# A decoder layer on one core: its first block done by batch entry, its first latents without transfers

## The chip, the cores and the metric

The kernel runs on one NeuronCore of a Trainium2 chip. The metric is device time in microseconds of one execution; lower is better. The engines are TensorE (PE: matmuls; its weight loads are shown as PEld), VectorE (DVE), ScalarE (ACT) and GpSimd (POOL). Each takes its instructions strictly in the order in which they were issued, and they meet through semaphores. Most DMA transfers are issued by SyncE (SP), also in order; a few are issued by ScalarE.

## The reference

One decoder layer over x of 32 batch entries, 256 tokens, 256 features, all float32. In short:

```python
x = x + attn(layernorm(x))               # causal self attention
x = x + xattn(layernorm(x), ctx, mask)   # cross attention
x = x + ffn(layernorm(x))                # relu, fp8-quantised hidden values
```

Self attention goes through latents: `q = (x @ Wqa @ Wqb)` with 64 latents, `kv = (x @ Wkva @ Wkvb)` with 32, 16 query heads of 16 features, 4 key and value heads, rotary positions on q and k, a causal softmax, then `@ Wout + bout`. Cross attention takes keys and values from `ctx`, 16 heads of 16 features, and a mask of 256 x 256. Scores are held to float32 accuracy: operands are split into a rounded high half and a low remainder ("halves"), each multiplied for itself.

## The kernel before

The 32 batch entries are worked on two at a time: 16 blocks (i = 0 to 15) of 512 tokens. Each block has a self attention (a0, a1, ...), a cross attention (x0, x1, ...) and a feed-forward part. An attention is a job of 8 units; a unit is one batch entry b and one group g of four heads. The jobs run one behind the other: a0, a1, x0, a2, x1, a3, ... , a15, x14, x15. So between a0 and x0 there is only a1 to cover a0's output projection, norm, transposes and x0's queries.

The order of instructions is written out by hand. Time is counted in steps, one unit to a step: at step s the maxima of unit s are computed (`row_max`: scores by TensorE, masked maximum by VectorE, line 400), two units earlier is weighted (`weigh`: scores again with the maximum subtracted; `exponential` on ScalarE; for self attention GpSimd zeroes the upper triangle), and every second step the values of an earlier pair are summed (`values`, copied to `num`, and spread by `gather`: denominators to `den`, outputs to `oT`). Dense work is hung between them by `at(pos, fn, rank)`, where pos is a step in halves, and rank 1 comes after rank 0. All engines and SP's queue follow this one order.

An attention's units run g outside and b inside, unless the job stands in `APART`; then b is outside, so that the first four units need only batch entry 0. `APART` held a15, x14 and x15. For i = 15 the tail of the self attention is then also done by entry (`divide_entry`, `tr_entry`, `xquery_entry`, `queries_entry`), for the other blocks over both entries at once (`divide`, `tr`, `xquery`, `queries`).

The path in front of the first scores: x of block 0 is loaded; `Norm.moments` (VectorE, then GpSimd), `Norm.scaled` (ScalarE), transposes to `xnT` (`tr`), and `lat`: one product with `wa_sb` gives 96 rows of latents, ScalarE copies them to `rlat` and rounds them, GpSimd makes the low halves, and six SP transfers spread them over 128 partitions as `lk` and `lq` (lines 680 and 684). `rotated` multiplies by the weights with rotary pairs (`rope`: TensorE, VectorE line 349, GpSimd line 350), `split` makes halves again (lines 335 and 336), and `keys` and `queries` spread them by transfers (`spread`, line 294) to the tiles that the units read. For a0 the second of each two groups is issued by ScalarE, the rest by SP. Each of the 512 tokens of the block goes through each of these in one piece.

Tiles come from small rings: `hl` (halves) has three buffers, `r` and `t` two, the PSUM pool of dense work two banks, that of the scores three pairs; `lk`, `lq`, `xn` and `den` have one buffer each.

Positions of block 0: the load at -16, moments -14 and -13.5, norm -13 and -12.5, transposes -12, latents -11, keys -9 and 0.5, queries -8 and 1.5 (each for one half of the features, both entries), values 2.5; reciprocal of the denominators 11.5, divide 12.5, output projection 13 and 13.5, norm 13.5 and 14, transposes 14.5, x0's queries 15 and 15.5, x0 itself from 16.

Of the kernel before, what the change touches and what calls it, by code (L numbers as in the profile page):

```python
# [10 lines left out]
F32 = mybir.dt.float32  # L11
F32R = mybir.dt.float32r
# [5 lines left out]
ALU = mybir.AluOpType  # L18
# [23 lines left out]
def decoder_layer(  # L42
# [3 lines left out]
    w_a, w_q, w_k, w_v, w_out, b_out,  # L46
# [25 lines left out]
    def load(name, src):  # L72
        return fetch(const.tile(list(src.shape), src.dtype, name=name), src)
# [18 lines left out]
    wa_sb = load("wa_sb", w_a)  # L92
    bout_sb = load("bout_sb", b_out)
# [4 lines left out]
    low_sb = load("low_sb", low)  # L98
    ones2_f = fetch(sm.tile([P, 2, P], F32, tag="nmT", name="ones2_f"), ones2)
# [14 lines left out]
    def latent_weights():  # L114

        nc.scalar.copy(wq_s[0], wq_f)
        nc.gpsimd.tensor_tensor(wq_s[1], wq_f, wq_s[0].bitcast(F32), ALU.subtract)
        for w, f in ((wk_s, wk_f), (wv_s, wv_f)):
            hi = sm.tile(list(f.shape), F32R, tag="t", name="hi_w")
            nc.scalar.copy(hi, f)  # L120
            nc.vector.scalar_tensor_tensor(w, hi.bitcast(F32), low_sb, f, ALU.mult, ALU.add)

    def score_constants():


        nc.vector.tensor_copy(ones2_sb, ones2_f)
        nc.gpsimd.tensor_copy(sel_sb, sel_f)

        tri_f = sm.tile([P, S], F32, tag="t", name="tri_f")
        nc.gpsimd.memset(tri_f, 0.0)  # L130
        nc.gpsimd.affine_select(
            out=tri_f, in_=tri_f, compare_op=ALU.is_ge, fill=NEG_CAUSAL,
            base=P, pattern=[[-1, S]], channel_multiplier=1,
        )
        nc.vector.tensor_copy(causal_qk, tri_f)

# [154 lines left out]
    def spread(job, t, part, e):  # L291

        queue = nc.scalar if job.first and e == 1 else nc.sync
        queue.dma_start(out=t, in_=part[e * 64 : (e + 1) * 64])

    def queries(job, c, hl):

        for e in range(2):
            g = 2 * c + e
            t = act.tile([P, TOK], F32R, tag=f"q{g}{job.set}", name=f"q{g}_{job.name}", bufs=1)  # L300
            rows = t.bitcast(F32).rearrange("(r s) t -> s r t", s=2)
            for s in range(2):
                spread(job, rows[s], hl[:, s, :].bitcast(F32), e)
            job.q[g] = t
# [15 lines left out]
    def keys(job, c, hl):  # L320

        for e in range(2):
            g = 2 * c + e
            t = act.tile([P, 2, TOK], F32R, tag=f"k{g}{job.set}", name=f"k{g}_{job.name}", bufs=1)
            rows = t.bitcast(F32).rearrange("(r s) h t -> s r h t", s=2)
            for s in range(2):
                spread(job, rows[s], hl.bitcast(F32), e)
            job.k[g] = [t[:, h, :] for h in range(2)]
# [4 lines left out]
    def split(name, r, n=P):  # L333
        hl = halves(name)
        nc.scalar.copy(hl[:n, 0, :], r[:n])
        nc.gpsimd.tensor_tensor(hl[:n, 1, :], r[:n], hl[:n, 0, :].bitcast(F32), ALU.subtract)  # L336
        return hl
# [25 lines left out]
    class Job:  # L363
        def __init__(self, name, n, causal, apart):
            self.apart = apart
            self.units = [(g, b) for b in range(2) for g in range(G)] if apart else [
                (g, b) for g in range(G) for b in range(2)
            ]
            self.name, self.set, self.causal, self.first = name, n % 2, causal, n == 0
            self.q, self.k = {}, {}  # L370
            self.mx, self.nmT, self.wT = {}, {}, {}
# [176 lines left out]
    APART = {("a", NI - 1), ("x", NI - 2), ("x", NI - 1)}  # L548
# [17 lines left out]
    def entries(i):  # L566
# [28 lines left out]
        def tr(name):  # L595
# [5 lines left out]
            return run  # L601

# [205 lines left out]
        if i == 0:  # L808
            p = dict(load=-16, m=(-14, -13.5), n=(-13, -12.5), tr=-12, lat=-11, k=(-9, 0.5), q=(-8, 1.5), v=2.5)
        elif i == 1:  # L810
# [5 lines left out]
        at(s0 + p["load"], load)  # L816
        for c in range(2):
            ln("a", c, s0 + p["m"][c], s0 + p["n"][c], s0 + p["n"][c])
        at(s0 + p["tr"], tr("a"))
        at(s0 + p["lat"], lat)  # L820
        for c in range(EC):
            for kind in "kq":
                rotated(kind, c, s0 + p[kind][c])
        at(s0 + p["v"], value)

        if i in (0, NI - 1):
            p = dict(inv=11.5, div=(12.5, 12.5), o=(13, 13.5), n=(13.5, 14), tr=14.5, q=(-1, -0.5), k=(-5, -4), ctx=-8, v=(3.5, 4))
            if i == NI - 1:
                p.update(inv=(8, 12), div=(9.5, 13.5), o=(10.5, 14.5), n=(11.5, 15.5), tr=(12, 16), q=(-3, 1), k=(-7, -1))
            if i == 0:  # L830
                p.update(ctx=-13, v=(-2, 0))
# [26 lines left out]
        if jx.apart:  # L858
# [26 lines left out]
    at(-11.5, latent_weights)  # L885
    at(-9.5, score_constants)
# [62 lines left out]
def _constants():  # L949
# [12 lines left out]
    low = np.zeros((P, 1), np.float32)  # L962
    low[2 * KVL :] = -1.0
# [6 lines left out]
def _layout(a):  # L970
# [6 lines left out]
        "w_a": _chunks(np.concatenate([a["L0_attn_Wqa"], a["L0_attn_Wkva"]], axis=1)),  # L977
        "w_q": np.tile(_both(a["L0_attn_Wqb"]), (2, 1, 1)),
# [38 lines left out]
```

## Time and profile before

| | us |
|---|---|
| median of three runs | 1688.2 (1687.71 to 1691.75) |
| the profiled execution | 1687.51 |
| its span, from first to last instruction | 1685.8 |
| first scores on TensorE | 33.36 |
| first masked maximum of a0, a1, x0, a2 | 34.6, 89.9, 164.3, 208.5 |
| the next jobs, each | 46.9 to 48.6 |
| granted TensorE clock, mean | 0.951 |

A page of the profile has busy times of each engine, and forty slices of the span in which a digit is the busy share in tenths; `PEclk` is the clock that TensorE was granted, in tenths of full speed. A line of the timeline has the start, the duration, the engine (`SPq` is SP's queue), the line of the kernel, the operation, the tile written and those read, the shape, how many in a row, and in brackets how long the engine had been idle and what ended that. A line of waits has the engine, the tile and line that waited, what it waited for, the total in us, how often, and the longest. The span is 2.4 us shorter than the median.

### The profile page before, as it was taken

The page shows a single profiled execution, that of the slowest core. Times are in us where ns is not written, and L with a number is a line of the kernel's source. Part 1 is how long each engine was busy: PE and PEld are TensorE (multiplying, and loading weights), DVE is VectorE, ACT ScalarE, POOL GpSimd, SP SyncE. Part 2 cuts the span into 40 slices and gives each one's busy share as a digit, 9 for nine tenths or more (in the row PEclk, how much of TensorE's full clock was granted, in tenths as well). Part 3 has the DMA queues.
Part 4 walks back from the last instruction along what each step waited for, and adds up shares of the span by engine and source line. Part 5 has one row for each costly group of instructions (what it writes and reads, how often), then busy time and mean ns, then how long its engine had stood idle before and what let it go on. Part 6 is the DMA issues. An engine that isn't in the chain of part 4 may idle for free. (4 is left out here: it accounts for less than half of the span.)

```text
span 1685.8 us, 47975 instructions
## 1 busy us (share of the span) xinstructions
PE 1540.7 (91%) x17748; PEld 1002.2 (59%) x17748; DVE 1291.0 (77%) x5083; ACT 964.2 (57%) x1545; POOL 1099.8 (65%) x1862
## 2 busy tenths in 40 slices
PE   3777899999999999999999999999999999989886
PEld 2444566665656566665656566665656566555664
DVE  3554978979797888879787887878787887957861
ACT  2343566666665666666566666656566666545542
POOL 5655576776867677685867677675867677555521
PEclk7687799999999999999999999999999999999898
DMA  4533234252434335242434325243434425131200
GB/s 137 169 97 95 78 84 129 62 136 66 113 92 125 96 77 149 65 125 77 114 86 125 102 68 158 59 110 96 114 90 114 112 63 135 52 89 46 61 18 22
DMA packets 85738, 160.42 MB, mean 95 GB/s; under 512 B 15296, under 2 KB 36160, under 8 KB 85376
## 3 DMA queue, kind: packets, MB, share of 16 engines
q1 hardware_dynamic: 84864, 155.78, 34.6%
q8 instruction: 140, 2.29, 0.6%
q10 hardware_dynamic: 640, 1.57, 0.3%
q14 instruction: 94, 0.77, 0.1%
HBM read 22.03 MB, written 8.39 MB: 18 GB/s over the span
## 5 line engine op out<-in xcount | busy, mean ns | idle before, releaser
L400 DVE CUSTOM_DVE_ANT_0 ms_x<-s_x,mb_qk 128x256 f32<-128x256 f32 x1024 | 362.0, 417 | 64.2 <-POOL hl_q L336 23.9
L400 DVE CUSTOM_DVE_ANT_0 ms_a<-s_a,causal_qk 128x128 f32<-128x128 f32 (+1 forms) x1024 | 294.3, 352 | 61.3 <-PE s_a L389 17.8
L430 DVE TENSOR_TENSOR wT_x<-wT_x,cap_kq 128x1024 f32<-128x1024 f32 x256 | 303.4, 1225 | 0.0
L455 ACT ACTIVATE wT_x<-s_x 128x1024 f32<-128x1024 f32 x256 | 248.3, 1023 | 30.5 <-PE s_x L442 30.2
L405 POOL CAST maxima<-m_x 128x8 fp32r<-128x8 f32 x128 | 115.6, 903 | 214.7 <-DVE m_x L400 113.2
L775 PE MATMUL ps_h<-xnT_f,w_sb 128*128 128x512 f32 x448 | 221.4, 616 | 0.0
L455 ACT ACTIVATE wT_a<-s_a 128x768 f32<-128x768 f32 x256 | 193.3, 807 | 23.5 <-PE s_a L442 19.5
L461 POOL TENSOR_SCALAR_AFFINE_SELECT wT_a<-wT_a 128x256 f32<-128x256 f32 x512 | 191.6, 411 | 21.2 <-ACT wT_a L455 21.1
L389 PE MATMUL s_a<-k_a,q_a 32*128 32x128 f32 (+1 forms) x2048 | 115.8, 314 | 35.1 <-ACT wT_a L455 19.5
L442 PEld LDWEIGHTS s_a<-q_a,k_a 32*128 32x128 f32 x2048 | 86.6, 189 | 80.3 <-issue 66.4
L779 ACT ACTIVATE hq<-ps_h,b_sb 128x512 fp8e4<-128x512 f32 x112 | 77.1, 689 | 91.6 <-PE ps_h L775 91.6
L479 PE MATMUL av_x<-wT_x,v_cross 128*32 128x256 f32 x2048 | 129.2, 393 | 0.0
L389 PE MATMUL s_x<-k_x,q_x 32*128 32x256 f32 x2048 | 111.4, 311 | 17.9 <-ACT wT_x L455 8.8
L442 PEld LDWEIGHTS s_x<-q_x,k_x 32*128 32x128 f32 x2048 | 81.7, 187 | 76.0 <-issue 62.0
L389 PEld LDWEIGHTS s_x<-k_x,q_x 32*128 32x128 f32 x2048 | 79.3, 188 | 74.2 <-issue 32.3
L389 PEld LDWEIGHTS s_a<-k_a,q_a 32*128 32x128 f32 x2048 | 82.3, 195 | 67.6 <-ACT wT_a L455 23.0
L442 PE MATMUL s_a<-q_a,k_a 32*128 32x256 f32 (+1 forms) x2048 | 112.8, 295 | 10.3 <-DVE m_a L400 9.4
L775 PEld LDWEIGHTS ps_h<-xnT_f,w_sb 128*128 128x128 f32 x448 | 76.0, 189 | 73.5 <-issue 54.4
L479 PE MATMUL av_a<-wT_a,v_self 128*32 128x256 f32 (+1 forms) x2048 | 109.9, 361 | 9.0 <-DVE t_k L349 9.0
L442 PE MATMUL s_x<-q_x,k_x 32*128 32x256 f32 x2048 | 115.0, 308 | 2.8 <-DVE m_x L400 2.8
L405 POOL CAST maxima<-m_a 128x8 fp32r<-128x8 f32 x128 | 63.4, 495 | 77.8 <-DVE m_a L400 75.4
L486 ACT COPY num_a<-av_a 128x512 f32<-128x512 f32 x64 | 37.5, 586 | 106.2 <-PE av_a L479 105.9
(173 smaller groups left out, 3298.5 us busy)
## 6 DMA issues: line engine op xcount, KB each, us to landing
k_x<-hl_xk SPq DMA_DIRECT2D x128, 256.0 KB
k_a<-hl_k SPq DMA_DIRECT2D x124, 256.0 KB
q_a<-hl_q SPq DMA_DIRECT2D x124, 128.0 KB
q_x<-hl_xq SPq DMA_DIRECT2D x120, 128.0 KB
x<-in_x SPq DMA_DIRECT2D x16, 512.0 KB
ctxT<-in_ctxT SPq DMA_DIRECT2D x16, 512.0 KB
out_y<-x SPq DMA_DIRECT2D x32, 256.0 KB
oT_a<-num_a SPq DMA_DIRECT2D x60, 128.0 KB
```

The source lines that it names most:

```text
L389: nc.tensor.matmul(pts[j // 2][:, j % 2, c * S : c * S + w], job.q[g][r : r + HB, b * S + c * P : b * S + (c + 1) * P], k_[r : r + HB, b * ...
L400: nc.vector.tensor_tensor_reduce(ms[:, :w], pts[j // 2][:, j % 2, c * S : c * S + w], causal_qk[:, S - w :] if job.causal else mb_qk[:, c, :],
L405: nc.gpsimd.tensor_copy(mx[:, :, :, o], m)
L430: nc.vector.tensor_tensor(wT, wT, cap, ALU.min)
L442: nc.tensor.matmul(pts[j // 2][:, j % 2, c * S : c * S + S - q0], job.k[g][n][r : r + HB, kc] if n < 2 else ones2_sb[r : r + HB, u % 2, :] ...
L455: nc.scalar.activation(wT[:, :, :n], pt[:, :, :n], AF.Exp, scale=SCALE)
L461: nc.gpsimd.affine_select(out=o, in_=o, compare_op=ALU.is_ge, fill=0.0, base=0, pattern=[[0, 2], [1, P]], channel_multiplier=-1,)
L479: nc.tensor.matmul(av[j * HB : (j + 1) * HB, n * S + q0 : (n + 1) * S], job.v[:, 2 * b + c, head, :], wTs[j // 2][:, j % 2, c * S : c * S ...
L486: nc.scalar.copy(num, av)
L775: nc.tensor.matmul(ps, w1_sb[:, c, f * P : (f + 1) * P], st["xnT"][:, c, :], start=(c == 0), stop=(c == EC - 1),)
L779: nc.scalar.activation(st["hq"][:, f, :], ps, AF.Relu, bias=b1_sb[:, f : f + 1], saturate=False)
```

## The change

Block 0 gets a front of its own, by batch entry, and a0 and x0 join `APART`:

```diff
-    APART = {("a", NI - 1), ("x", NI - 2), ("x", NI - 1)}
+    APART = {("a", 0), ("x", 0), ("a", NI - 1), ("x", NI - 2), ("x", NI - 1)}
```

Its latents come from TensorE already spread over 128 partitions, by a weight tile with the columns repeated (`w_a0`, 128 x 512 instead of 128 x 192), and their halves are made in place: ScalarE rounds, and VectorE adds the product, from which `low_sb` (now two columns) takes the rounded part away in those rows that hold low halves. No transfer is used:

```diff
+        def lat_one(b):
+            def run():
...
+                ps = mm_bank(f"ps_lat_{i}_{b}")
+                for m in range(2):
+                    for c in range(EC):
+                        nc.tensor.matmul(
+                            ps[:, m * S : (m + 1) * S], wa0_sb[:, c, m, :],
+                            st["xnT"][:, c, columns(b)], start=(c == 0), stop=(c == EC - 1),
+                        )
+                for m, l in enumerate(("lk", "lq")):
+                    hi = sm.tile([P, S], F32R, tag="t", name=f"hi_{l}_{b}")
+                    nc.scalar.copy(hi, ps[:, m * S : (m + 1) * S])
+                    nc.vector.scalar_tensor_tensor(
+                        st[l][:, columns(b)], hi.bitcast(F32), low_sb[:, 1 - m : 2 - m],
+                        ps[:, m * S : (m + 1) * S], ALU.mult, ALU.add,
+                    )
```

The order of block 0's front, entry 0 ahead of the units, entry 1 among them:

```diff
+            at(-17, score_constants)
+            at(-16, load)
+            at(-15, lambda: moments(0))
+            at(-14.5, lambda: moments(1))
+            at(-14.5, lambda: st["norm", "a"].scaled(0), 1)
+            at(-14, key_weights)
+            at(-13.5, tr_entry("a", 0, "xnT"))
+            at(-13, query_weights)
+            at(-12.5, lat_one(0))
+            at(-12, lambda: st["norm", "a"].scaled(1), 1)
+            at(-11.5, rotated_one("k", 0, 0))
+            at(-11, rotated_one("q", 0, 0))
+            at(-10.5, halved("k", 0, 0))
+            at(-10, halved("q", 0, 0))
+            at(-9.5, spread_one("k", 0, 0, (0,), nc.sync))
+            at(-9.5, spread_one("q", 0, 0, (0,), nc.sync))
+            at(-9, tr_entry("a", 1, None))
+            at(-8.5, spread_one("k", 0, 0, (1,), nc.scalar))
+            at(-8.5, spread_one("q", 0, 0, (1,), nc.scalar))
+            at(-8, rotated_one("k", 1, 0))
+            at(-7.5, rotated_one("q", 1, 0))
+            at(-7, maxima_rows)
+            for n, kind in enumerate("kq"):
+                at(-6.5 + n / 2, halved(kind, 1, 0))
+                at(-6 + n / 2, spread_one(kind, 1, 0, (0, 1), nc.sync), 1)
+            at(0, lat_one(1))
+            for n, (kind, c) in enumerate((("k", 0), ("q", 0), ("k", 1), ("q", 1))):
+                at(0.5 + n, rotated_one(kind, c, 1))
+                at(1 + n, halved(kind, c, 1), 1)
+                at(1 + n, spread_one(kind, c, 1, (0, 1), nc.sync), 1)
+            at(1, lambda: halves_of(wv_s, wv_f))
+            at(2, value)
+            at(2.5, reciprocal_rows)
+            for b in range(2):
+                at(6 + b, lambda b=b: raised(st["x"], b, bout_sb), 1)
```

`score_constants` now holds only the causal mask; `maxima_rows` and `reciprocal_rows` are the other two constants, `key_weights`, `query_weights` and `halves_of(wv_s, wv_f)` the three parts of what was `latent_weights`. `raised` adds the output bias to x on GpSimd; before it followed `scaled`. `split`, `keys` and `queries` take an entry and work on its 256 columns alone, so a spread of block 0 is two transfers of half the size. On SP's queue the loads now stand in the order x, `wa0_sb`, `wk_f`, `wq_f`, `cs_sb`, `wv_f`, `low_sb`, `wa_sb`, `bout_sb`.

The tail of a0 is done by entry, at the places that block 15 already had:

```diff
         if i in (0, NI - 1):
-            p = dict(inv=11.5, div=(12.5, 12.5), o=(13, 13.5), n=(13.5, 14), tr=14.5, q=(-1, -0.5), k=(-5, -4), ctx=-8, v=(3.5, 4))
-            if i == NI - 1:
-                p.update(inv=(8, 12), div=(9.5, 13.5), o=(10.5, 14.5), n=(11.5, 15.5), tr=(12, 16), q=(-3, 1), k=(-7, -1))
+            p = dict(inv=(8, 12), div=(9.5, 13.5), o=(10.5, 14.5), n=(11.5, 15.5), tr=(12, 16), q=(-3, 1), ctx=-8, k=(-7, -1), v=(3.5, 4))
             if i == 0:
-                p.update(ctx=-13, v=(-2, 0))
+                p.update(ctx=-13, k=(-5, -4), v=(-2, 0))
```

x0's units run b outside; its own tail stays as it was, over both entries (`if jx.apart` became `if i >= NI - 2`). In `gather` an `APART` job spreads its outputs by two transfers to a pair, not one, and fills `den` with ones first.

## The prediction

> **What bounds the kernel now.** I read the page's slices first, then the waits of TensorE, then the timeline at each wait, then a table of windows.
>
> ```profile
> span 1685.8 us, 47975 instructions
> PE 1540.7 (91%) x17748; PEld 1002.2 (59%) x17748; DVE 1291.0 (77%) x5083; ACT 964.2 (57%) x1545; POOL 1099.8 (65%) x1862
> PE   3777899999999999999999999999999999989886
> PEclk7687799999999999999999999999999999999898
> ```
>
> From slice 7 on TensorE is full: nothing is to be won there, except by starting it earlier. Slices 1 to 5 (0 to 210 us) are not full, and their clock is below full speed too. The change touches only these. The first masked maximum of each attention on VectorE marks the stages: a0 at 34.6, a1 at 89.9, x0 at 164.3, a2 at 208.5 us. So a0 takes 55.3, a1 74.4 and x0 44.2 us, where later ones take 47 to 48 with more dense work in them.
>
> The start, from the timeline:
>
> ```profile
> 14.85 0.58 ACT L675 COPY rlat<-ps_lat 96x512 f32<-96x512 f32 x1 [1.24 <-PE ps_lat L668]
> 16.10 3.13 SPq L680 DMA_DIRECT2D lk<-hl_lat  x4
> 19.27 1.24 SPq L684 DMA_DIRECT2D lq<-hl_lat  x2
> 20.77 1.19 PE L344 MATMUL ps_r_k<-lk,wk_s 128*128 128x256 f32 x4 [5.96 <-DMA lk<-hl_lat]
> 28.18 1.95 SPq L294 DMA_DIRECT2D q_a<-hl_q  x2
> 33.36 1.23 PE L389 MATMUL s_a<-k_a,q_a 32*128 32x128 f32 x16 [8.93 <-DMA q_a<-hl_q]
> ```
>
> Six transfers spread the latents, 5.96 us of TensorE idle; later the queries' spread costs 8.93 us more. The first scores start at 33.36.
>
> The a1 stage, by waits of TensorE (88 to 164 us) and by windows (columns: PE, PEld, DVE, ACT, POOL busy, granted clock, DMA share, GB/s):
>
> ```profile
> PE s_x L389 <- DMA q_x<-hl_xq: 7.3, 1, 7.3
> PE s_a L442 <- DVE m_a L400: 6.7, 2, 5.4
> PE ps_T_x L284 <- ACT xn_x L269: 2.9, 1, 2.9
> ```
>
> ```profile
> 115.50:120.80 5.30, 0.00 (x0) 0.00 (x0) 2.80 (x10) 0.87 (x2) 0.00 (x0) 0.92 0.71 162
> 120.80:130.60 9.80, 8.47 (x80) 6.08 (x81) 6.00 (x28) 2.40 (x4) 5.68 (x12) 0.52 0.28 71
> 130.60:142.50 11.90, 10.08 (x100) 7.78 (x98) 6.89 (x28) 4.14 (x9) 6.88 (x13) 1.00 0.85 207
> 142.50:151.20 8.70, 5.83 (x56) 3.72 (x56) 2.68 (x18) 4.16 (x8) 5.96 (x15) 0.61 0.33 84
> 155.60:162.90 7.30, 0.02 (x5) 0.04 (x4) 0.00 (x0) 1.19 (x2) 4.60 (x9) 0.86 0.25 56
> 162.90:207.20 44.30, 38.25 (x482) 26.61 (x482) 39.14 (x148) 19.56 (x29) 23.11 (x36) 0.75 0.28 73
> ```
>
> Here a0's tail (reciprocal, projection, norm, transposes, x0's queries) runs as one chain for both batch entries and ends just as x0 wants its queries: three stalls, 5.3, 2.9 and 7.3 us, and after each a stretch at half clock.
>
> **The change part by part.**
>
> *Latents (first scores).* I walk the new order with old durations. The causal mask's cast now stands ahead of the moments on VectorE and waits for GpSimd (memset done at 4.11, then 0.30 + 0.21 + 0.40), cast 0.29: moments start at 5.3, not 4.71. So the normalised pair ends at 8.71 + 0.6 = 9.3; three transposes of 0.30 after it: 10.4; ScalarE copy 0.59: 11.05. Latents, four matmuls of 256 columns: half of the 3.19 for four of 512, 1.6: 12.7. Rounding 0.39 (the 128x256 cast of nmT) and the low half by VectorE, half of 1.34: lk at 13.0, lq at 13.9. Query rotation 1.05 (half of eight matmuls in 2.05), VectorE 0.69, GpSimd sum 0.73: 16.6. GpSimd then makes the low halves of keys and queries, half of 1.26 each: 17.25 and 17.9. SP issues two key transfers (1.1) and two of queries, the last from 18.9. Landing: before 3.8 us from the last issue (29.55 to 33.36) with the DMA engines full; 4 KB transfers landed 1.7 us after theirs (116.3 to 118.0). Half the bytes lie between; I take 2.8: 21.7. Gain 33.4 - 21.7 = **11.6**, bounds 12.7 and 8.5 (the latter if all of the longer landing and 2 us of queueing on ACT or low_sb's load come on top). Six transfers, a 0.58 copy, a 0.62 cast and a 1.26 subtraction are gone; the larger latent weights (256 KB instead of 96) are second in SP's queue behind x and wanted only at 11.
>
> [...]
>
> *a0's own steps.* Entry 1's latents, rotations, splits and spreads now lie among units 0 to 3. Extra on VectorE: two low halves, 1.34, and the value weights, 0.27; on TensorE 1.9 (half of the 3.73 that a1's latents took at half clock); on ScalarE two roundings of 0.39 and four casts of 0.39 for two of 0.62, less the issue of four transfers (2 us). The bias additions (two of 1.27, GpSimd) move from 9.24 us into steps 6 and 7. Rotations: as many in these steps as before. VectorE and TensorE take turns here, so I charge VectorE's 1.6 and some queueing: **+2**; bounds -2 (all covered: TensorE was busy 41.7 of these 55.4 us) and +6 (all of it in series at half clock). Entry 1's keys are wanted only at unit 4, three steps after their split.
>
> *SP's queue.* It gains 30 transfers: 20 key and query spreads of a0, 8 of x0's queries, 8 of outputs, less the 6 of the latents. At 0.55 each, 16.5 us. Between 20 and 170 us SP stood waiting for its producers some 89 us: covered, unless an in-order wait holds a1's latents back.
>
> *a0's tail and x0's queries by entry.* Entry 0's reciprocal moves from step 11.5 to 8, and its queries' spread from step 15.5 to 13.5, against use at 16; entry 1's comes at 17.5 against use at 20. The 7.3 us wait goes: **-7.3** (bounds -7.3, -2 if the eight smaller transfers are still in flight). The 5.4 us wait came from VectorE's reciprocal, held since den stood behind lk's transfers on SP, which waited for the values' matmul. That order stays, but the reciprocal now stands behind the next unit's maxima (2.3 us, ready): left 2 of 5.4, **-3.4** (bounds -5.4, 0). The transposes' 2.9 becomes two waits, one an entry; the same code in the last block waited 0.5 on ScalarE, its steps fuller; I take 1 each: **-0.9** (-2.9, +1.5). The second reciprocal (1.74), its rounding (0.40) and remainder (0.72) fall on engines half idle here.
>
> *Clock.* After the stalls TensorE was busy 8.5, 5.8 and (162.9 to 167.5, without a gap) 4.6 us at half clock; half of that, 9.4, is extra. Without the long gaps I take **-7** (bounds -9.4, and -2 if the small waits that are left drop it as well).
>
> [...]
>
> *x0.* Four transposes and eight query matmuls of entry 1 come into it, some 2 us that leave a1: 0 in sum (0, +2). From a2 on the order is as before.
>
> Sum: -11.6 + 2 - 7.3 - 3.4 - 0.9 - 7 = **-28.2**. The profiled span, 1685.8, becomes 1657.6. The median shown, 1688.2, is 2.4 above that span, so **1660**. All good ends give -40, all bad ones -3.
>
> **Rivals.**
> - *a0 eats the front's gain.* a0's steps are bound by their chain over five engines, not by when they start, and ScalarE, in order, holds unit work behind splits that wait for a free buffer (three, each free when its spread has landed). For: a0 ran at clock 0.62 and 10.8 us went between units 2 and 3. Against: the loads are issued relative to the steps and move along. a0 at +11: 1669.
> - *The stall only moves.* x0's later units, or the reciprocal, wait in place of the first: the tail's 18.6 falls to 5: 1674. Against: 2.5 steps of some 5.5 us are left each time.
> - *Slower.* SP goes in order; if each of the 28 spreads that it now issues for a0 waits for the one before to land (1.7 + 0.55 against 0.55), that is +48, less 28: 1708; it decides from 17 such waits on. Against: before, SP issued back to back at 0.5 us with several in flight.
> - *The change isn't in the built order.* The order of the built instructions shows the latents' six transfers gone and a0 and x0 by entry; dismissed.
>
> **Numbers.** Forecast (1648 to 1665) 0.62; a0 eats it 0.14; the stall moves 0.12; slower 0.05; no difference beyond 0.3% (about 5 us, what a measurement can tell) 0.03; a gain beyond 40 us 0.04. Range 1647 to 1678. Faster 0.92, same 0.03, slower 0.05.
>
> **What would show it.** First scores near 21.7 and the moments at 5.3; a0's eight units in about 57 us; a1's in 56; no wait of TensorE over 3 us for q_x, and clock 1.00 over most of a1; from a2 to the end a time unchanged within 2 us. Wrong if a0's units take over 62, if a query wait of x0 shows up at its fifth unit, or if SP's spreads start long after their low halves are done.

## The result and the profile after

The changed kernel takes 1658.84 us (median of four, 1656.61 to 1660.33) where the kernel before, timed with it, takes 1687.95 (1686.73 to 1691.75): ratio 0.9823, 95% interval 0.9803 to 0.9843. The forecast was 1660. Repeated later (`after_again` below) it took 1661.35 (ratio 0.985, 0.9829 to 0.9872); over all nine times the median is 1659.82.

From the page of the kernel after, the span, TensorE's totals and its two rows of slices:

```profile
span 1656.1 us, 48107 instructions
PE 1533.5 (93%) x17768; PEld 1000.1 (60%) x17768; DVE 1298.1 (78%) x5088; ACT 965.6 (58%) x1554; POOL 1100.6 (66%) x1868
PE   4797899999999999999999999999999999989886
PEclk8788899999999999999999999999999999999898
```

TensorE's 1540.7 us of busy time fell by only 7; the span fell by 29.7. So about three quarters of the gain, 22.5 us, is idle time that is gone, and 26.5 us of the gain lie ahead of a2, in slices 0 to 4. The first masked maximum on VectorE marks the beginning of each job, as in the table before:

| | before | after | difference of the stage | forecast |
|---|---|---|---|---|
| first scores on TensorE | 33.36 | 24.72 | -8.6 | -11.6 |
| first maximum of a0 | 34.6 | 26.0 | | |
| a0, to a1's first maximum | 55.3 | 56.7 | +1.4 | +2 |
| a1, to x0's | 74.4 | 52.7 | -21.7 | -18.6 |
| x0, to a2's | 44.2 | 46.6 | +2.4 | 0 |
| a2, to a3's | 48.6 | 47.3 | -1.3 | 0 |

The start, from the timeline of the kernel after (columns as before):

```profile
5.07 0.42 DVE L269 BATCH_NORM_STATS2 stats_a<-x 128x6 f32<-128x256 f32 x1
10.70 3.78 PE L627 MATMUL ps_lat<-xnT_a,wa_sb 128*128 128x256 f32 x8 [0.67 <-ACT xnT_a L711]
14.52 0.37 ACT L633 CAST hi_lk<-ps_lat 128x256 fp32r<-128x256 f32 x1 [3.35 <-PE ps_lat L627]
14.93 0.48 DVE L634 SCALAR_TENSOR_TENSOR lk<-hi_lk,low_sb,ps_lat 128x256 fp32r<-128x256 f32 x1 [4.56 <-ACT hi_lk L633]
15.46 0.80 PE L357 MATMUL ps_r_k<-lk,wk_s 128*128 128x256 f32 x2 [0.98 <-DVE lk L634]
21.30 1.20 SPq L302 DMA_DIRECT2D q_a<-hl_q  x2
24.72 1.23 PE L402 MATMUL s_a<-k_a,q_a 32*128 32x128 f32 x16 [3.47 <-DMA q_a<-hl_q]
```

No transfer stands between the product and the first rotation any more, and TensorE's wait there went from 5.96 to 0.98 us. But the product takes 3.78 us, and ScalarE's rounding of the first half waits until the whole of it is done.

The a1 stage, by waits of TensorE from 82 to 136 us, and by windows (us, length, then busy time of PE, PEld, DVE, ACT, POOL, the granted clock, the DMA share and GB/s):

```profile
PE s_x L402 <- DVE stats_a L269: 4.4, 1, 4.4
PE s_a L402 <- DMA q_a<-hl_q: 2.5, 1, 2.5
PE s_a L455 <- DVE m_a L413: 0.6, 1, 0.6
PE ps_T_x L707 <- ACT xn_x L278: 0.5, 2, 0.4
```

```profile
82.00:106.00 24.00, 22.14 (x276) 14.79 (x276) 15.35 (x76) 13.35 (x23) 17.18 (x37) 0.86 0.33 81
106.00:129.00 23.00, 21.24 (x240) 14.43 (x244) 13.56 (x64) 12.00 (x24) 17.97 (x31) 0.93 0.68 162
129.00:134.00 5.00, 0.65 (x24) 0.50 (x20) 2.16 (x12) 3.06 (x5) 1.79 (x6) 0.74 0.77 223
```

The waits of 5.4 and 2.9 us are gone; that for x0's queries shrank from 7.3 to 4.4. From 82 to 129 us TensorE is busy 43.4 of 47 us. The name in the first line misleads: L402 there waits for x0's query transfers as well, and VectorE's moments of a3 had to wait for a load that SP sent just ahead of those transfers. SP's queue shows both (start, duration of the issue):

```profile
127.41 1.12 SPq L69 DMA_DIRECT2D x<-in_x  x1
128.63 5.75 SPq L326 DMA_DIRECT2D q_x<-hl_xq  x8
```

Over the stage (89 to 164.3 us before, 82 to 135.4 after) TensorE's busy time fell from 51.85 to 45.39 us, and its idle time from 23.4 to 8.0. The products are not quite the same: of x0's, entry 1's four transposes and half of the columns of the query products now come after the stage.

### The profile page after: what moved, and what is told of

It is laid out like the page before. It is cut to its first block, busy times and chain, and to the rows that moved or that the text cites. A ratio compares the mean times of both kernels' runs of the same rounds, so it can differ in the third digit from the quotient of the medians.

```text
span 1656.1 us, 48107 instructions
## 1 busy us (share of the span) xinstructions
PE 1533.5 (93%) x17768; PEld 1000.1 (60%) x17768; DVE 1298.1 (78%) x5088; ACT 965.6 (58%) x1554; POOL 1100.6 (66%) x1868
## 5 line engine op out<-in xcount | busy, mean ns | idle before, releaser
L418 POOL CAST maxima<-m_x 128x8 fp32r<-128x8 f32 x128 | 119.0, 930 | 206.5 <-DVE m_x L413 103.2
L402 PE MATMUL s_a<-k_a,q_a 32*128 32x128 f32 (+1 forms) x2048 | 114.7, 310 | 31.0 <-ACT wT_a L468 16.7
L455 PEld LDWEIGHTS s_a<-q_a,k_a 32*128 32x128 f32 x2048 | 84.9, 187 | 73.4 <-issue 66.1
L402 PE MATMUL s_x<-k_x,q_x 32*128 32x256 f32 x2048 | 112.0, 311 | 15.0 <-ACT wT_x L468 8.1
L402 PEld LDWEIGHTS s_x<-k_x,q_x 32*128 32x128 f32 x2048 | 79.4, 188 | 71.0 <-issue 19.0
L402 PEld LDWEIGHTS s_a<-k_a,q_a 32*128 32x128 f32 x2048 | 81.2, 191 | 63.9 <-ACT wT_a L468 20.0
L455 PE MATMUL s_x<-q_x,k_x 32*128 32x256 f32 x2048 | 115.5, 308 | 2.7 <-DVE m_x L413 2.7
L492 PE MATMUL av_a<-wT_a,v_self 128*32 128x256 f32 (+1 forms) x2048 | 104.8, 349 | 9.3 <-DVE t_k L362 9.2
L418 POOL CAST maxima<-m_a 128x8 fp32r<-128x8 f32 x128 | 63.8, 498 | 63.2 <-DVE m_a L413 60.8
```

What stands on the lines that cost most here:

```text
L402: nc.tensor.matmul(pts[j // 2][:, j % 2, c * S : c * S + w], job.q[g][r : r + HB, b * S + c * P : b * S + (c + 1) * P], k_[r : r + HB, b * ...
L418: nc.gpsimd.tensor_copy(mx[:, :, :, o], m)
L455: nc.tensor.matmul(pts[j // 2][:, j % 2, c * S : c * S + S - q0], job.k[g][n][r : r + HB, kc] if n < 2 else ones2_sb[r : r + HB, u % 2, :] ...
L492: nc.tensor.matmul(av[j * HB : (j + 1) * HB, n * S + q0 : (n + 1) * S], job.v[:, 2 * b + c, head, :], wTs[j // 2][:, j % 2, c * S : c * S ...
```

## The experiments

All numbers in one table: medians, ratios to the kernel before with their intervals, stages of the profiled execution in us (up to the next job's first maximum), and the time between 20 and 240 us that TensorE was granted half clock (added up from windows).

| | us | ratio | first maximum of a0 | a0 | a1 | x0 | a2 | half clock |
|---|---|---|---|---|---|---|---|---|
| before | 1687.95 | | 34.6 | 55.3 | 74.4 | 44.2 | 48.6 | 107 |
| after | 1658.84 | 0.9823 (0.9803-0.9843) | 26.0 | 56.7 | 52.7 | 46.6 | 47.3 | 65 |
| tail_whole | 1677.56 | 0.9933 (0.9907-0.9958) | 25.9 | 57.2 | 75.6 | 43.7 | 50.5 | 85 |
| latents_sent | 1664.09 | 0.9853 (0.9831-0.9874) | 28.7 | 55.5 | 52.0 | 46.9 | 50.3 | 51 |
| front_whole | 1665.44 | 0.9863 (0.9841-0.9885) | 30.2 | 58.4 | 53.4 | 47.9 | 46.9 | 82 |
| filler | 1661.14 | 0.9839 (0.9815-0.9864) | 26.0 | 56.9 | 52.8 | 44.9 | 51.7 | 65 |
| x0_whole | 1672.47 | 0.991 (0.9896-0.9923) | 25.6 | 57.1 | 66.0 | 44.7 | 50.1 | 83 |
| load_later | 1658.79 | 0.983 (0.9817-0.9844) | 26.1 | 57.5 | 50.3 | 47.4 | 50.2 | 68 |
| w1_later | 1661.27 | 0.984 (0.9827-0.9854) | 25.5 | 55.4 | 53.1 | 47.7 | 50.4 | 75 |
| best1 | 1656.1 | 0.9815 (0.9802-0.9829) | 24.4 | 55.5 | 50.6 | 47.5 | 49.1 | 72 |
| after_again | 1661.35 | 0.985 (0.9829-0.9872) | 25.2 | 56.5 | 52.2 | 46.1 | 50.4 | 72 |
| best1_again | 1656.39 | 0.9811 (0.9794-0.9829) | 24.7 | 54.8 | 49.3 | 46.8 | 49.1 | 66 |
| x0_late | 1662.64 | 0.985 (0.9835-0.9864) | 25.5 | 55.2 | 55.8 | 45.4 | 50.2 | 83 |
| recip_early | 1667.64 | 0.9882 (0.9866-0.9898) | 25.9 | 56.6 | 62.9 | 47.6 | 50.4 | 85 |

The first three expectations give 24.7 us as the changed kernel's first maximum of a0; that is its first scores, and the first maximum is at 26.0. Below, like is compared with like. Each row's stages are those of one execution. The two of the changed kernel, `after` and `after_again`, differ by 0.8 us at a0's first maximum, by 0.5 in a1's and x0's stages and by 3.1 in a2's, so a difference of that size between two rows may be chance.

### The tail over both entries again: tail_whole

```diff
-    APART = {("a", 0), ("x", 0), ("a", NI - 1), ("x", NI - 2), ("x", NI - 1)}
+    APART = {("a", 0), ("a", NI - 1), ("x", NI - 2), ("x", NI - 1)}
...
-                p.update(ctx=-13, k=(-5, -4), v=(-2, 0))
+                p.update(inv=11.5, div=(12.5, 12.5), o=(13, 13.5), n=(13.5, 14), tr=14.5, q=(-1, -0.5), ctx=-13, k=(-5, -4), v=(-2, 0))
...
-        if ja.apart:
+        if i == NI - 1:
```

> Undoes the second half of the change alone: a0's averages, division, projections and moments, x0's queries and x0's eight units go over both entries again, in the old order; front and first scores stay as changed. My theory (the split tail is worth what the stage from a1's first maximum to x0's first maximum lost, 74.4 to 52.7 us): first maximum of a0 at 24.7-25 and of a1 at 82 +-1, stage of a1 back to 74 +-4 us, TensorE's long waits there (q_x over 5 us, reciprocal over 4 us) back, time 1680 +-5. Rival (that stage gained from the earlier start and from fewer clock cuts, and the split of the tail is worth little): stage of a1 under 60 us, time 1667 or less.

It took 1677.56 us, with the a1 stage at 75.6. TensorE's waits from 83 to 160 us:

```profile
PE s_x L402 <- DMA q_x<-hl_xq: 7.2, 1, 7.2
PE s_a L455 <- DVE m_a L413: 6.9, 2, 6.3
PE ps_T_x L293 <- ACT xn_x L278: 2.8, 1, 2.8
```

All three stalls of the kernel before are back at nearly their old length, though a1 began 6.8 us earlier than there. So the stage's gain comes from the tail, not from the earlier start. The rival falls. 18.7 of the 29.1 us are the tail's (17.7 against the median of all nine times), x0's order by entry included, since this run undoes it too.

### The first latents by transfers again: latents_sent

```diff
+                if b == 0:
+                    n = QL + KVL
+                    for c in range(EC):
+                        nc.tensor.matmul(
+                            ps[:n, :S], wa_sb[:, c, :], st["xnT"][:, c, :S],
+                            start=(c == 0), stop=(c == EC - 1),
+                        )
...
+                    hl = split(f"lat_{i}", r, n, b=0).bitcast(F32)
+                    for s in range(4):
+                        nc.sync.dma_start(
+                            out=st["lk"].bitcast(F32)[s * KVL : (s + 1) * KVL, :S], in_=hl[QL:n, s % 2, :S]
+                        )
```

(and two more for `lq`; `wa_sb` and `wa0_sb` change places in the order of loads.)

> Puts the transfers back for the latents of entry 0 alone: one 96-row product, its copy and halves, and six transfers of 64 KB in place of four 128-row products and two combinations in place. My theory (the transfers overlap one another, and their landing of 2-2.8 us comes in the place of 1 us of longer product and 1 us of combination): lk and lq ready near 18.3 us in place of 16.3, first maximum of a0 at 26.7 (25.7 to 28.7) in place of 24.7, time 1661 (1660 to 1663). Rival (the whole of TensorE's idle stretch before the first rotated product, some 6 us in the kernel before, is the transfers' price): first maximum at 29.5 to 30, time 1664.

The timeline of its start:

```profile
10.69 2.02 PE L628 MATMUL ps_lat<-xnT_a,wa_sb 128*96 128x256 f32 x4 [0.68 <-ACT xnT_a L730]
13.57 2.58 SPq L636 DMA_DIRECT2D lk<-hl_lat  x4
17.54 0.77 PE L357 MATMUL ps_r_k<-lk,wk_s 128*128 128x256 f32 x2 [4.83 <-DMA lk<-hl_lat]
19.01 0.55 PE L357 MATMUL ps_r_q<-lq,wq_h 128*128 128x256 f32 x1 [0.71 <-DMA lq<-hl_lat]
```

The rotation of the keys begins 2.1 us later than with the latents made in place (17.54 to 15.46), that of the queries 2.6 later (19.01 to 16.38), the first scores 2.7 later (27.40 to 24.72). So of the 5.96 us that TensorE stood in the kernel before, taking the transfers away wins 2.1 to 2.7, near my theory's 2 and not the whole. TensorE's wait ahead of the keys' rotation is 4.83 us here and 0.98 there, but the product takes 2.02 here and 3.78 there, and so 1.8 of the 3.9 us are paid back. The time is 5.3 us up, 4.3 against the median of all nine. The front explains 2.7 of it; a2's stage took 50.3 in place of 47.3, but it took 50.4 in the changed kernel's second execution too.

Another thing can be read here: this execution had no half clock at all between 20 and 57 us, where the changed kernel had it from 32.4 to 49.4. Its a0 stage, with 14 us of half clock in place of 27, was only 1.2 us shorter; that of the kernel before, with 41, took 55.3. So a0's length does not follow TensorE's clock in these runs.

### Both entries ahead of the first scores: front_whole

```diff
+                at(-12.5, lat_one(b))
+                at(-11.5, rotated_one("k", 0, b))
...
+                at(-9.5, rotated_one("q", 0, b))
...
-            at(0, lat_one(1))
-            for n, (kind, c) in enumerate((("k", 0), ("q", 0), ("k", 1), ("q", 1))):
-                at(0.5 + n, rotated_one(kind, c, 1))
```

> Undoes the first half by entry: both entries' latents, keys and queries are made before the first scores, without transfers for the latents; the tail stays by entry. My theory (half of the work in front of the first scores is only moved behind them, so the stage of a0 gives some of it back): first maximum of a0 at 30 (28.5 to 31.5) in place of 24.7, stage of a0 (its first maximum to a1's) 54.5 in place of 56.7, time 1662 (1660 to 1664). Rival A (pure shift, nothing given back): stage of a0 unchanged at 56.7, time 1664 to 1665. Rival B (work behind the first scores costs a0 all of it): stage of a0 51.5, time 1659.

First scores in its timeline:

```profile
28.82 1.36 PE L402 MATMUL s_a<-k_a,q_a 32*128 32x128 f32 x18 [2.84 <-DMA q_a<-hl_q]
```

They are 4.1 us later than in the changed kernel, and the time is 1665.44. a0's stage was not shorter for the work taken out of it, but 1.7 us longer. My theory, that a0 would give back half, falls; rival A is nearest: the work of entry 1 costs a0 nothing where it lies among the units. The half clock that this execution had from 26 to 57 us can be a part of the 1.7; that was not separated.

So of the 8.6 us by which the first scores came earlier, 2.7 go with the transfers and 4.1 with the entries; 1.9 are left for the rest of the new order and the two together. The first scores of the changed kernel's second execution came at 23.97, so each of these is good to some 0.8 us.

### TensorE kept busy ahead of x0: filler

```diff
+    def filler():
+        ps = mm_bank("ps_fill")
+        for k in range(4):
+            nc.tensor.matmul(ps, ident, cs_sb.rearrange("p m s -> p (m s)"), start=True, stop=True)
...
+    at(15.5, filler, 1)
```

> Adds four products whose result is not used, some 3.8 us of TensorE, placed where TensorE stands idle from 129.6 to 134.0 us ahead of x0's first scores. My theory (that idle stretch is what cuts the granted clock in half from 131 to 138 us, and x0's stage pays for it): granted clock over 131-139 us near 1.00 in place of about 0.5, stage of x0 44.3 in place of 46.6, time 1657 (-2 against the changed kernel). Rival (the half clock there costs nothing, x0's beginning is bound by VectorE or by the transfers): stage of x0 46.6 +-0.5, time unchanged or up by 1.

Windows of this kernel, with the changed kernel's one window of half clock in its a2 stage below them:

```profile
129.00:134.00 5.00, 4.32 (x32) 1.99 (x28) 1.77 (x10) 3.10 (x5) 1.79 (x6) 1.00 0.74 200
134.00:139.00 5.00, 4.18 (x54) 3.35 (x54) 4.37 (x22) 1.53 (x4) 3.12 (x9) 1.00 0.60 139
180.60:203.20 22.60, 19.76 (x250) 12.91 (x250) 19.42 (x81) 14.54 (x25) 16.34 (x24) 1.00 0.31 74
203.20:213.40 10.20, 9.88 (x100) 7.54 (x100) 7.56 (x35) 4.30 (x8) 5.50 (x13) 0.50 0.11 30
223.60:227.00 3.40, 3.40 (x39) 1.89 (x34) 2.31 (x16) 0.54 (x2) 2.86 (x7) 0.51 0.91 254
```

```profile
206.40:209.80 3.40, 3.40 (x32) 2.95 (x32) 3.26 (x14) 1.99 (x4) 0.41 (x2) 0.51 0.11 39
```

The first step is as expected: the clock stays at 1.00 over 129 to 139 us and x0's stage is 1.7 us shorter. But the time is not. In a2's stage there are 13.6 us of half clock in place of 3.4, and that stage is 4.4 us longer. Over 20 to 240 us the half clock adds up to 65 us in both. But the changed kernel's second execution, without these products, has 10.2 us of half clock in a2's stage and 50.4 us for it. So it is not shown that the products moved the half clock there. What the times show (1661.14 for 1659.82) is that products without use do not pay here.

### x0 over both entries, the tail by entry: x0_whole, recip_early, x0_late

The first of the three changes a0's entry 1 as well, since its queries must stand ahead of x0's first unit:

```diff
-                p.update(ctx=-13, k=(-5, -4), v=(-2, 0))
+                p.update(inv=(8, 11), div=(9.5, 12.5), o=(10.5, 13.5), n=(11.5, 14), tr=(12, 14.5), q=(-3, -1), ctx=-13, k=(-5, -4), v=(-2, 0))
```

with `("x", 0)` taken out of `APART`.

> Keeps a0's averages, division, projections and moments by entry, with those of entry 1 one to one and a half units earlier, but x0's eight units go over both entries again, so that both entries' queries stand ahead of its first unit. My theory (the wait for x0's queries is a part of its own, some 7 us, and only x0's order by entry shortens it): TensorE's wait ahead of x0's first scores 8 to 11 us in place of 4.4, stage of a1 59 (57 to 62) in place of 52.7, time 1665 (1662 to 1668). Rival (the reciprocal and the tail in halves carry the whole gain of that stage, x0's order none of it): stage of a1 53 +-1, time 1659 +-2.

The a1 stage took 66.0 us. Neither theory has it: the wait for x0's queries was 3.1 us, less than in the changed kernel, and TensorE stood 10.8 us for something else, the normalised pair of entry **0**, whose steps had not been moved. 8.5 us were lost by a1's fifth unit already, long before x0. The suspect was entry 1's reciprocal, one unit earlier. So it was moved alone, with x0 by entry:

```diff
-                p.update(ctx=-13, k=(-5, -4), v=(-2, 0))
+                p.update(inv=(8, 11), ctx=-13, k=(-5, -4), v=(-2, 0))
```

> Moves one step only: entry 1's reciprocal of a0 one unit earlier (11 in place of 12); all else, x0 by entry included, as in the changed kernel. Theory (VectorE goes in order, and the averages' transfer stands on SP behind the latents' transfers, which wait for the values' product: the reciprocal holds everything behind it on VectorE until 111.4 us): VectorE idle some 9 us before the reciprocal, TensorE's wait for entry 0's normalised pair 10 to 11 us in place of 0.4, stage of a1 61 (59 to 63), time 1667 (1665 to 1669). Rival (half a tail leaves enough other work, the unit's place does not matter): stage 53 +-1, time 1659 to 1661.

Its timeline:

```profile
104.92 2.50 SPq L776 DMA_DIRECT2D lk<-hl_lat  x4
109.39 1.14 SPq L512 DMA_DIRECT2D den_a<-num_a  x2
111.76 1.74 DVE L528 RECIPROCAL rec_a<-den_a 32x256 f32<-32x256 f32 x1 [9.22 <-DMA den_a<-num_a]
116.28 1.09 ACT L278 ACTIVATE xn_x<-x,shift_x,rstd_x 128x256 f32<-128x256 f32 x2 [2.29 <-POOL shift_x L274]
116.94 1.39 PE L707 MATMUL ps_T_x<-ident,xn_x 128*128 128x128 f32 x4 [10.60 <-ACT xn_x L278]
```

Read it upwards from the last line. TensorE waits 10.6 us for a normalised pair; its moments stand on VectorE behind a reciprocal that waited 9.22 us; its averages come by a transfer that stands on SP behind a2's latents, which wait for the values' product. The same reciprocal in the kernel before and in the changed one, and what SP waited for ahead of the latents in each:

```profile
118.00 1.74 DVE L515 RECIPROCAL rec_a<-den_a 32x256 f32<-32x256 f32 x1 [8.60 <-DMA den_a<-num_a]
SPq L680 <- PE ps_v L705: 11.7, 1, 11.7
```

```profile
111.37 1.74 DVE L528 RECIPROCAL rec_a<-den_a 32x256 f32<-32x256 f32 x1 [3.23 <-DMA den_a<-num_a]
SPq L776 <- PE ps_v L801: 11.2, 1, 11.2
```

In the changed kernel it begins as late as in recip_early, but only 3.2 us of VectorE's time are lost to it, since the moments stand ahead. The theory holds, with the stage at 62.9 and the time at 1667.64: **one instruction one unit too early on an in-order engine costs 8 us** (against 1659.82). The stage of the one profiled execution shows more, 10.2 us; that execution took 1672.47, the longest of the four, where the others took 1667.42 to 1667.8.

Then x0 over both entries with that reciprocal where the changed kernel has it:

```diff
-                p.update(ctx=-13, k=(-5, -4), v=(-2, 0))
+                p.update(inv=(8, 12), div=(9.5, 13), o=(10.5, 13.5), n=(11.5, 14), tr=(12, 14.5), q=(-3, -0.5), ctx=-13, k=(-5, -4), v=(-2, 0))
```

> As the run before with x0's units over both entries, but entry 1's reciprocal stays where the changed kernel has it (unit 12 of the count) and its division, projection and moments follow at once. There the reciprocal, one unit earlier, stood on VectorE from about 102 to 111.4 us waiting for its averages and held back entry 0's residual; 8.5 of its 13.3 us were lost by a1's fifth unit. Theory (the rest, some 5 us, is what x0's order by entry is worth): a1's fifth first maximum near 105.6 as in the changed kernel, TensorE's wait ahead of x0's first scores 6 to 10 us, stage of a1 58 (56 to 61), time 1664 (1661 to 1667). Rival A (x0's order is worth nothing by itself): stage 53 +-1, time 1660. Rival B (it is worth the whole 13): stage 65 or more, time 1671.

```profile
PE s_x L402 <- DMA q_x<-hl_xq: 3.7, 1, 3.7
PE ps_T_x L707 <- ACT xn_x L278: 3.3, 3, 2.8
```

These are its waits from 82 to 150 us. The stage took 55.8 us, just under the theory's range, and the wait for x0's queries was not 6 to 10 but 3.7. So x0's order by entry is worth some 3 us of this stage, not 5 and not the 7 of my prediction. In the time it is 2.8 us (1662.64 for 1659.82), which is not clear of noise: the ratio, 0.985 (0.9835 to 0.9864), is that of after_again.

With these, the gain of the a1 stage can be followed by unit. First maximum of a1's units and of x0, counted from a1's first:

| | unit 2 | 3 | 4 | 5 | 6 | 7 | 8 | x0 |
|---|---|---|---|---|---|---|---|---|
| before | 5.0 | 12.3 | 17.2 | 29.8 | 37.7 | 48.3 | 58.6 | 74.4 |
| tail_whole | 4.7 | 11.4 | 16.3 | 29.9 | 37.8 | 49.2 | 59.5 | 75.6 |
| recip_early | 5.3 | 12.1 | 17.7 | 32.0 | 42.1 | 48.9 | 55.7 | 63.0 |
| x0_late | 5.7 | 11.4 | 17.0 | 22.8 | 31.4 | 40.3 | 49.0 | 55.8 |
| after | 5.6 | 11.4 | 17.1 | 22.9 | 31.5 | 38.2 | 44.7 | 52.7 |

Before to after: 6.9 us by unit 5, where the reciprocal held VectorE; 7.0 more by unit 8, over which the projection, the norm and the transposes of both entries had gone in one chain; 7.8 more from unit 8 to x0, where the kernel before waits 7.3 us for x0's queries.

### What is left: load_later, w1_later, best1

One step each: a3's input load behind x0's queries, and the fetch of the first feed-forward weights three units later.

```diff
+            if i == 3:
+                p.update(load=-25.5, m=(-22, -21))
```

> Moves one step only: the input load of a3 (512 KB) goes on SP's queue behind x0's first query transfers in place of ahead of them. My theory (VectorE's moments of a3 and the transfers of x0's queries both wait for that load): query transfers sent from about 127.4 in place of 128.6, TensorE's wait ahead of x0's first scores 1.5 to 2.5 us in place of 4.4, first maximum of x0 at 133 in place of 135.4, time 1656 (1655 to 1658). Rival A (x0's beginning is bound by the transfers themselves): wait 3.5 or more, time 1659. Rival B (the wait shrinks, but clock cuts move to a later stage, as they did with the added products): first maximum of x0 at 133, stage of a2 50 to 52 in place of 47.3, time 1659 to 1661.

```diff
-    at(6, lambda: fetch_later("w1", "b1"))
+    at(9, lambda: fetch_later("w1", "b1"))
```

> Moves one step only: the fetch of the first feed-forward weights goes three units later. My theory (TensorE's 2.5 us wait for a query copy at a1's first unit, at 82 us, comes from that fetch standing ahead of the copies in the queues): that wait under 1 us, stage of a0 54 to 55 in place of 56.7, time 1656 (1655 to 1658). Rival (the copies are late for another reason, or the gain goes into clock cuts placed elsewhere): wait 2 us or more or a later stage longer by as much, time 1658 to 1661.

The first fence has two waits of load_later from 82 to 136 us: x0's, and the one at a1's first unit, which this step leaves as it was (2.5 us in the changed kernel). The second is from w1_later's waits, 20 to 185 us. Under that name the changed kernel has two waits, 3.5 us at the first scores and 2.5 at a1's first unit:

```profile
PE s_x L402 <- DMA q_x<-hl_xq: 2.1, 1, 2.1
PE s_a L402 <- DVE w_q L247: 2.1, 1, 2.1
```

```profile
PE s_a L402 <- DMA q_a<-hl_q: 4.2, 1, 4.2
```

Both remove what they were to remove: the wait ahead of x0 is 2.1 us (a1's stage 50.3 for 52.7), and only the first scores' wait for a query copy is left (a0's stage 55.4 for 56.7). Both times are nevertheless those of the changed kernel, 1658.79 and 1661.27: x0 and a2 together took 97.6 and 98.1 us in place of 93.9. Rival B of the one and the rival of the other come nearest. But x0 and a2 took 96.5 in the changed kernel's second execution, so most of the longer x0 and a2 may be chance, and where these gains went is not shown.

best1 has both steps and a PSUM bank for each of the first two latent products:

```diff
-                ps = mm_bank(f"ps_lat_{i}_{b}")
+                ps = [mm_bank(f"ps_lat{m}_{i}_{b}") for m in range(2)]
...
-                            ps[:, m * S : (m + 1) * S], wa0_sb[:, c, m, :],
+                            ps[m][:, :S], wa0_sb[:, c, m, :],
```

> Both moves of steps together, and the two products of the first latents in a bank each, so that the first is rounded while the second runs (first maximum of a0 at 25.1 in place of 26.0). My theory (the three gains add up: 0.9, 2.5 and 3 us): time 1653 (1651 to 1656). Rival (TensorE's clock cuts take the place of the stalls taken away, whose sum from 20 to 240 us stayed at 32 us of full-speed time in the run with added products): time 1657 to 1661, with the half-speed time moved and not shorter.

```profile
12.81 0.37 ACT L633 CAST hi_lk<-ps_lat 128x256 fp32r<-128x256 f32 x1 [1.64 <-PE ps_lat L627]
13.84 0.58 PE L357 MATMUL ps_r_k<-lk,wk_s 128*128 128x256 f32 x2
23.18 1.23 PE L402 MATMUL s_a<-k_a,q_a 32*128 32x128 f32 x16 [4.40 <-DMA q_a<-hl_q]
```

From its timeline: the first rounding begins at 12.81 for 14.52, while the second product runs, and the first scores come 1.5 us earlier than in the changed kernel's first profile, 0.8 earlier than in its second. At x0's first maximum it is 4.9 us ahead of the changed kernel's first profile. The time is 1656.1 us: neither the sum of the three gains (1653) nor nothing.

### The same two once more: after_again, best1_again

> The changed kernel once more, beside the combined version on the same chip. Theory (TensorE's half-speed stretches lie on a grid of 3.4 us that stands differently to the work in every execution, and so decide where a few us are lost from x0 on): first maxima of a0, a1 and x0 within 0.5 us of 26.0, 82.7 and 135.4, edges of the half-speed stretches again multiples of 3.4 us apart but shifted against the work, the stages of x0 and a2 together 93.9 + or - 3, time 1658 to 1661. Rival (the stretches belong to the program and repeat): the same edges within 0.3 us, x0 46.6 and a2 47.3 within 0.3.

> The combined version once more, beside the changed kernel on the same chip. Theory (two of the 4.9 us that it is ahead of the changed kernel at x0's first maximum stay to the end): 1656 +-1 and 2 to 3 us below the changed kernel's median in the same runs. Rival (the whole lead goes into half-speed stretches): within 1 us of the changed kernel.

The first fence has windows of the changed kernel's first profiled execution, the second of this one:

```profile
128.00:131.40 3.40, 1.65 (x48) 1.13 (x36) 2.73 (x18) 2.10 (x3) 1.52 (x6) 1.00 0.88 239
131.40:138.20 6.80, 4.17 (x26) 3.67 (x27) 3.90 (x21) 2.05 (x4) 4.10 (x12) 0.50 0.64 172
```

```profile
130.00:133.40 3.40, 0.52 (x16) 0.55 (x16) 1.39 (x6) 1.98 (x4) 1.38 (x4) 0.99 0.71 228
133.40:136.80 3.40, 3.40 (x19) 2.85 (x16) 3.05 (x18) 0.96 (x2) 2.89 (x9) 0.51 0.51 113
```

The same instructions, but half clock for 6.8 us at x0's first scores in the one execution and 3.4 in the other; in a2's stage 3.4 in the one and 10.2 in the other. x0 and a2 together took 96.5 us for 93.9, with 72 us of half clock in all for 65. The rival falls. Of the theory's numbers two are off: the first maxima of a0, a1 and x0 moved by 0.8, 1.0 and 1.5 us, not 0.5, and the time is 0.35 us above its range. So one profile does not tell differences of that size from chance.

best1_again took 1656.39 us beside 1661.35 for the changed kernel: ratios 0.9811 (0.9794 to 0.9829) and 0.985 (0.9829 to 0.9872). Over all times of each the medians are 1656.1 (of eight) and 1659.82 (of nine). So it is the fastest version here, by some 4 us or 0.2%, where 2 to 3 were expected; the intervals of the two just touch.

## Why the prediction was right, and where it was not

**The total** was right: -28.2 forecast, -29.1 measured. It is partly luck: in the first profiled execution the errors are +3.0 us (first scores), -0.6 (a0), -3.1 (a1), +2.4 (x0), -1.3 (a2) and -1.9 (from a3 on), and nearly cancel; and within a1 the terms were shared out wrongly.

**First scores**: -11.6 forecast, -8.6 measured, at the weak end of the bounds (-8.5). The term that failed is the product: "half of the 3.19 for four of 512, 1.6". It took 3.78. The loop over `EC` issues two products, and the old row has x4 (as latents_sent's has): each is recorded twice. The new row's x8 is four products of 256 columns, a pair for the keys' latents and a pair for the queries'. Two of 512 columns or four of 256 are the same number of columns, so nothing was to be halved: 3.19 us before and 3.78 after, beside 2.02 for latents_sent's two of 256. `lk` was ready at 15.4 for 13.0 forecast, and the first scores came 3.0 late; 2.2 of these are the product's. The same slip halved entry 1's product in a0's term (1.9 for 3.51 measured). The other steps held nearly: moments at 5.07 (5.3 forecast), and the first scores 2.8 us after SP's last query transfer was issued (at 21.9, the second of the two from 21.30), where 2.8 was taken and the whole transfers before had 3.8. Whether the 1.0 us less comes from the size alone or from what else was in flight was not separated.

**a0's own steps**: +2 forecast, +1.4 measured. The rival "a0 eats the front's gain" falls. That the extra work on VectorE is what costs it was not shown: front_whole puts that work ahead of the first scores, and a0 did not get shorter.

**a0's tail**: the signs were right and the sum of the stage (-18.6 forecast with the clock's term, -21.7 measured) roughly, the parts not. The wait for x0's queries was priced at -7.3, gone entirely. It shrank by 2.9, and x0's order by entry, which was to remove it, is worth 3 us (x0_late). The reciprocal was priced at -3.4 since only TensorE's stall of 5.4 us was counted. But VectorE had stood 8.6 us, and what was queued behind it was late for all that follows: 6.9 us at unit 5, and 10 us of the stage (8 of the time) come back if that one instruction goes one unit earlier (recip_early). The transposes' -0.9 was -2.4: two waits of 0.5 us in all. Rival "the stall only moves" falls: by entry the tail has its stalls shorter, 4.4 us the longest.

**Clock**: -7 forecast, some -5 measured in the stage. TensorE's busy time there fell by 6.5 us, but not all of that is the clock's, since entry 1's transposes and query products left the stage. Of its busy time 20.2 us lay in windows of half clock before (92.6 to 99.4, 119.9 to 130.1, 143.8 to 150.6 and 160.9 to 164.3 us) and 10.4 after (83.6 to 90.4, 107.5 to 110.9 and 131.4 to 135.4); half of the difference, 4.9 us, is my estimate of what the clock gave (in the kernel before, a1's product of latents took 3.73 us at half clock, from 54.39 us, and a2's 1.90 at clock 1.00, from 102.34). "Clock 1.00 over most of a1" was too good as well: it was 0.86 over the first 24 us and 0.93 over the next 23.

**x0**: 0 forecast (0 to +2), +2.4 measured and +1.9 in the second execution. Where x0 goes over both entries, with the queries of entry 1 ahead of it, its stage took 43.7 to 45.4 us (before, tail_whole, x0_whole, x0_late; mean 44.5); by entry it took 44.9 to 47.9 (the ten other rows; mean 46.9). So the four transposes and four query products (eight in the trace) that came into it cost about 2.4 us, some of which the a1 stage no longer pays.

**SP's queue**: 0 forecast. A chain of spreads waiting for one another shows up nowhere: a0's stage is 1.4 us longer, where that rival had 48 us more, less 28. Rival "slower" falls. SP's order counts in another way, through the load ahead of x0's queries (a wait of 4.4 us, and 2.1 in load_later).

**From a2 on** a time unchanged within 2 us was forecast. The first profiled execution is 3.2 us shorter there than the kernel before (1474.1 for 1477.3 us), the second 0.3 longer. a2's own stage varies by 3 us between the two.

## What to carry to other kernels

A stall of the bounding engine is not the price of the instruction that it ends with: follow it to the engine that stood, count how long that engine stood and what was queued behind it, and put the waiting instruction behind whatever is ready; one place in the order was worth 8 us here. A chain over both halves of a tile ends in a stall at its end; by halves the second half's chain runs beside the first half's next work. That was worth 18.7 us here, of which 8 hang on the place of that one instruction and some 3 on the order of the next job. And when a product is laid out anew, count the columns of all its products, not the instructions of the old row (3.78 us here, where 1.6 was forecast).

## What the runs showed of the hardware

All edges of half clock in the changed kernel's profile between 20 and 240 us (32.4, 49.4, 56.2, 63.2, 73.4, 76.8, 83.6, 90.4, 107.4, 111.0, 131.4, 138.2 and so on to 209.8, read in windows of 0.2 us) lie whole multiples of 3.4 us apart (177.4 us from the first to the last, 52 steps of 3.41), and in after_again the grid stands elsewhere (34.4, 48.0, 54.8, 61.6). So in these two executions the clock changed in such steps only, and the steps lay differently against the work. a2's stage took 46.9 to 51.7 us over the kernels of the table from the changed one on, and where small stalls were taken away (filler, load_later, w1_later) there was no less half clock in all: 65, 68 and 75 us, beside 65 and 72 in the two executions of the changed kernel.

In the kernel before, TensorE's gap from 115.5 to 120.8 us has half clock from 119.9 to 130.1, and the gap of only 2.9 us up to 145.4 has it from 143.8 to 150.6. In the windows above, 1.65 us busy of 3.40 were followed by half clock, and in filler half clock lasted 10.2 us in which TensorE was busy for 9.88. What rule the clock follows, these runs do not settle.

Less half clock was not always less time: latents_sent had 51 us of it and took 4.3 us more than the changed kernel's nine times in the median, whose two profiles have 65 and 72; its later first scores explain 2.7 of the 4.3. a0's stage shows it best: 55.3, 56.7 and 55.5 us with 41, 27 and 14 us of half clock (before, after, latents_sent).
